# A selective-scan layer and an up-sampled MLP: sums of one pair in three a step later, and GpSimd's product by C in place, in one pool of six buffers

## The chip, the core and the metric

The kernel runs on one core of one Trainium2 chip, in float32 throughout. The time is that of one execution on the device, in microseconds (us), as the median of several runs. Five engines work side by side, each through its own queue in order: TensorE (PE in the profile; PEld is its load of weights), VectorE (DVE), ScalarE (ACT), GpSimd (POOL) and SyncE (SP), which issues the DMAs. They are held together by semaphores: an instruction starts when the counters that it names have reached their values.

## What is computed

Two layers on an image batch `x` of 8 x 64 x 64 x 96. The first normalises, projects to 192 channels, convolves, and runs a selective scan over the 4096 places of an image, in four directions (`K` = 4) and with 16 states for each channel. This is where nearly all the time goes:

```python
def step(h, inp):
    ul, dl, Bl, Cl = inp
    dA = jnp.exp(dl[..., None] * A)
    h = dA * h + (dl * ul)[..., None] * Bl[:, :, None, :]
    y = jnp.einsum('bkdn,bkn->bkd', h, Cl)
    return (h, y)
```

The four directions are added up, normalised, gated and projected back. The second layer is `x + conv(gn(x))`: an up-sampling by two through the frequencies, an MLP of 96, 384 and 96 channels with a quadratic in the middle, and a low-pass filter back to 64 x 64.

## The kernel before

**A tile** is one direction, 1024 places in a row, and 8 channels x 16 states = 128 partitions: a 128 x 1024 array. A chunk of 1024 places takes 24 tiles (`NT`), since 192 / 8 = 24; with 4 chunks, 4 directions and 8 images there are 3072 tiles, numbered through by the loop variable `i`. `t["i"]` is the place within the chunk, 0 to 23. Tiles whose place has remainder 2 by 3 are `by_pool`.

**What a tile goes through**, engine by engine:

- `fetch` (L1063, SyncE's queue): a DMA brings `dub`, the product of step and input, each channel copied to its 16 states (4 buffers).
- `product_b` (L1069, GpSimd): `bb = dub * br`, with B spread over the partitions (4 buffers).
- `decay` (L1075 on TensorE, L1082 on ScalarE): two matmuls spread the steps into `pd` in PSUM (2 buffers), and an exponential on ScalarE turns it in place into the decay.
- `scan` (L1089, VectorE): the recurrence itself. It writes over `pd`, or, where the tile is `by_pool`, into `h` in SBUF, of which there are 2 buffers.
- `product_c` (L1095): `hc = h * cr`. On VectorE right after the scan, or on GpSimd for the tiles `by_pool`. Both draw `hc` from one pool of 4 buffers.
- `hold` (L1108): the last column is copied to `carry` for the next chunk, by VectorE, or by ScalarE for the tiles `by_pool`. It is left out in the last chunk of a direction.
- `sums` (L1127, TensorE): the states are added up by matmuls with `sel_r` into `py`, one PSUM bank with one buffer. It is done for two tiles at a time, `a` and `a + 1` with `a` even, four matmuls in the source and eight in the profile, which has two records for each. After the pair with `j == 3` the earlier directions are added (L1139), ScalarE copies `py` out (L1160) and SyncE stores it.

**The order** is written by hand, with no scheduler: one pass of the loop at L1193 for each tile. In pass `i` the queues get: the fetch of tile `i + 6`; on GpSimd `product_c` of tile `i - 1` if it is `by_pool`, then `product_b` of tile `i + 3`; the decay of tile `i + 1`; the scan of tile `i`, then its `product_c` if it is VectorE's; its `hold`; a share of the side work; perhaps a filler matmul; and in odd passes the sums of the tiles `i - 3` and `i - 2`.

**Side work** is all that isn't the scan: the norms, convolutions, gates, projections, the MLP, and the preparation of the next chunk (`prepare`). `Side.advance` hands it out in small pieces, against a budget for each engine and pass (`CAPS`, 2.2 us of TensorE in a pass, up to 2.9 us saved up). The sums of a pair are charged to the budget of their pass as 0.95 us (`taken`). If less than 1.0 us of TensorE was given out in a pass, `turn_over` (L1101) adds a filler matmul into a spare bank.

**A cycle of six passes** therefore looks as follows, where a number is a tile's remainder by 6. Tiles 2 and 5 are GpSimd's. The pairs are (0, 1), (2, 3) and (4, 5). GpSimd gets the product of tile 5 in the next pass 0, and that of tile 2 in pass 3. TensorE gets, in this order: decay 2, sums of (4, 5) of the cycle before; decay 3; decay 4, sums of (0, 1); decay 5; decay 0, sums of (2, 3); decay 1. The sums of (4, 5) thus stand in front of decay 3, and need the product that GpSimd makes of tile 5.

Of the kernel before, what the change touches and what calls it, by code (L numbers as in the profile page):

```python
# [8 lines left out]
F32 = mybir.dt.float32  # L9
# [13 lines left out]
T = 1024  # L23
# [113 lines left out]
def kernel(ctx: ExitStack, tc: tile.TileContext, a: dict, out: bass.AP):  # L137
# [93 lines left out]
    sp = ctx.enter_context(tc.tile_pool(name="scan", bufs=3))  # L231
# [3 lines left out]
    side = Side(pss)  # L235
# [805 lines left out]
    tiles = []  # L1041
    for b in range(images):
        for k in (1, 0, 2, 3):
            order = range(NCH) if k < 2 else range(NCH - 1, -1, -1)
            for n, c in enumerate(order):
                got = {}
                for i in range(NT):
                    q, n8 = divmod(i, 8)
                    s, j = n8 % 2, n8 // 2
# [9 lines left out]
    def fetch(t):  # L1059
        assert t["got"]["ready"]  # L1060
        t["dub"] = sp.tile([128, T], F32, tag="dub", name="dub", bufs=4)
        g = t["g"]
        nc.sync.dma_start(  # L1063
            t["dub"], t["got"]["du"][None, 8 * g : 8 * g + 8, :].to_broadcast([NS, 8, T])
        )
# [18 lines left out]
    def scan(t):  # L1084
        step = 1 if t["k"] < 2 else -1
        pd = t["pd"]
        t["h"] = sp.tile([128, T], F32, tag="h", name="h", bufs=2) if t["by_pool"] else pd
        held = carry[:, t["g"] : t["g"] + 1]
        nc.vector.tensor_tensor_scan(  # L1089
            t["h"][:, ::step], pd[:, ::step], t["bb"][:, ::step], 0.0 if t["first"] else held, ALU.mult, ALU.add  # L1090
        )

    def product_c(t):
        t["hc"] = sp.tile([128, T], F32, tag="hc", name="hc", bufs=4)
        (nc.gpsimd if t["by_pool"] else nc.vector).tensor_tensor(t["hc"], t["h"], t["got"]["cr"], ALU.mult)  # L1095

    def turn_over():
# [14 lines left out]
    def parts(t):  # L1112

        o = y_dram[t["b"]][t["k"] % 2]
        q = t["q"]
        return [o[64 * q : 64 * q + 64, t["i0"] + MB * hf : t["i0"] + MB * hf + MB] for hf in range(2)]

    def sums(two):

        t0 = two[0]  # L1120
        if t0["j"] == 0:
            t0["got"]["py"] = psy.tile([128, MB], F32, tag="py", name="py")
        py = t0["got"]["py"]
        for t in two:
            for hf in range(2):
                r0 = 64 * hf + 32 * t["s"]
                nc.tensor.matmul(  # L1127
                    py[r0 : r0 + 32],
                    sel_r[:, t["j"], :],
                    t["hc"][:, MB * hf : MB * hf + MB],  # L1130
                    start=(t["j"] == 0),
                    stop=(t["j"] == 3 and t["k"] == 0),
                    skip_group_check=True,
                )

        if t0["j"] == 3 and t0["k"]:

            add = d_diag[:, t0["q"], :] if t0["k"] == 1 else ident
            nc.tensor.matmul(py, add, t0["got"]["yp"], start=False, stop=True, skip_group_check=True)  # L1139

    def before(t):

        if t["k"] == 0:
            return
        yp = t["got"]["yp"] = sp.tile([128, MB], F32, tag="yp", name="yp", bufs=2)
        if t["k"] == 1:
            q = t["q"]
            src = [
                u_dram[t["b"]][1][64 * q : 64 * q + 64, t["i0"] + MB * hf : t["i0"] + MB * hf + MB]
                for hf in range(2)  # L1150
            ]
        else:
            src = parts(t)
        for hf in range(2):
            nc.sync.dma_start(yp[64 * hf : 64 * hf + 64], src[hf])

    def store(t):
        yield dict(act=0.7)
        yq = sp.tile([128, MB], F32, tag="yq", name="yq", bufs=1)
        nc.scalar.copy(yq, t["got"]["py"])  # L1160
        yield {}
        for hf, part in enumerate(parts(t)):
            nc.sync.dma_start(part, yq[64 * hf : 64 * hf + 64])
        if t["q"] == Q3 - 1:
            if t["k"] == 3:
                summed.add((t["b"], t["i0"] // T))
            elif t["k"] == 2 and t["i0"] == 0:
                summed.add((t["b"], "even"))

    LEAD, FETCH = 3, 6  # L1170

    with tc.manual_schedule():
        side.queue = [bp.open("setup")]
        side.drain()
        constants_in()
        start, rest = front(0)
        side.queue = start[:-4]
        side.drain()
        side.queue = start[-4:] + [(8, 0, constants_of_scans), (8, 0, constants_of_mlp)]
        side.drain()  # L1180
        side.urgent = prepare(0, tiles[0]["k"], tiles[0]["i0"], tiles[0]["got"])
        side.queue, rest = rest[:4], rest[4:]
        while side.urgent or side.hurried:
            side.advance({e: (2 * most, 2 * most) for e, (_, most) in Side.CAPS.items()}, 2, 0)
        n = len(tiles)
        for i in range(FETCH):
            fetch(tiles[i])
            if i >= FETCH - LEAD:
                product_b(tiles[i - FETCH + LEAD])
        decay(tiles[0])  # L1190
        begin, *side.later = prepare(0, tiles[NT]["k"], tiles[NT]["i0"], tiles[NT]["got"])
        total = 1
        for i in range(n + 4):  # L1193
            t = tiles[i] if i < n else None
            at = i % (NT * NCH * K)
            if t and t["i"] == 0:
                b = t["b"]
                if at == 0:
                    y_dram[b] = [dr.tile([DI, L], F32, tag=f"y{o}", name=f"y{o}") for o in range(2)]
                    side.begun, hasty = 0, sum(item[1] for item in rest) if b == 0 else 0  # L1200
                    side.queue += rest
                    down, end = [], []
                    if b:
                        keep = {}
                        side.queue += tail(b - 1, keep)
                        up, down, end = mlp(b - 1, keep)
                        side.queue += up
                    if b + 1 < images:
                        start, rest = front(b + 1)
                        side.queue += start[:2] + [i for two in zip(down, start[2:10]) for i in two] if b else start[:10]  # L1210
                        side.queue += start[10:] + rest
                        rest = []
                    else:
                        side.queue += down
                    side.queue += end
                    total = sum(item[1] for item in side.queue)
                if b == images - 1 and at == NT * NCH * (K - 1):
                    keep = {}
                    side.queue += tail(b, keep, pairs=False)
                    total = 0  # L1220

            ahead = 4 if i < 2 * NT else 8
            if (i + ahead) % NT == 0 and i + ahead + NT < n:
                nxt = tiles[i + ahead + NT]
                begin, *side.later = prepare(nxt["b"], nxt["k"], nxt["i0"], nxt["got"])
                side.urgent.append(begin)

            if i == 2:
                side.urgent.append(begin)
            if i == 4 or i and i % NT == 0:  # L1230
                side.urgent += side.later
                side.later = []
            if t and t["i"] % 8 == 4:
                before(t)
            if i + FETCH < n:
                fetch(tiles[i + FETCH])
            if 0 < i <= n and tiles[i - 1]["by_pool"]:
                product_c(tiles[i - 1])
            if i + LEAD < n:
                product_b(tiles[i + LEAD])  # L1240
            if i + 1 < n:
                decay(tiles[i + 1])
            if t:
                scan(t)
                if not t["by_pool"]:
                    product_c(t)
                hold(t)
            ends = i % 2 == 1 and 3 <= i <= n + 2
            adds = ends and tiles[i - 2]["j"] == 3 and tiles[i - 2]["k"]
            side.advance(  # L1250
                Side.CAPS,
                2 if not total or side.begun < max(hasty, total * at / 290) else 0,
                0 if 7 <= i % NT <= 21 else 1,
                0.95 * (bool(ends) + bool(adds)),
            )
            turn_over()
            if ends:
                sums(tiles[i - 3 : i - 1])
                if tiles[i - 2]["j"] == 3:
                    side.stores.append([g := store(tiles[i - 2]), next(g)])  # L1260
        up, down, end = mlp(images - 1, keep)
        side.queue += up + down + end
        side.drain()
# [89 lines left out]
```

## Time and profile before

| what | value |
|---|---|
| runs (3) | 11121.33, 11125.21, 11125.94 us; median 11125.21 |
| the profiled execution | 11107.68 us, its span 11105.8 us |
| granted TensorE clock, mean | 0.982 |
| share of 16 DMA engines, queue of SyncE | 86.5% |
| ScalarE busy | 5910.6 us (53%) |
| scans, L1089, all four forms | 3072, 7163.7 us, 392.6 us idle before them |
| sums, L1127, matmuls | 12288 records, 1715.0 us |
| copies to `carry` by ScalarE, L1108 | 768, 172/182/193 ns (least/median/most) |

The span of a profile runs from the first to the last instruction; what lies around it is 1.9 us here. "Busy" is time in which an engine executes; "idle before" is the time that the engine stood before the instructions of a group, and the name behind the arrow is the instruction whose end let it go on, as inferred from the semaphores. A wait for several semaphores is put down to the one that came last.

### The profile page before, as it was taken

The page shows a single profiled execution, that of the slowest core. Times are in us where ns is not written, and L with a number is a line of the kernel's source. Part 1 is how long each engine was busy: PE and PEld are TensorE (multiplying, and loading weights), DVE is VectorE, ACT ScalarE, POOL GpSimd, SP SyncE. Part 2 cuts the span into 40 slices and gives each one's busy share as a digit, 9 for nine tenths or more (in the row PEclk, how much of TensorE's full clock was granted, in tenths as well). Part 3 has the DMA queues.
Part 4 walks back from the last instruction along what each step waited for, and adds up shares of the span by engine and source line. Part 5 has one row for each costly group of instructions (what it writes and reads, how often), then busy time and mean ns, then how long its engine had stood idle before and what let it go on. Part 6 is the DMA issues. An engine that isn't in the chain of part 4 may idle for free. (4 is left out here: it accounts for less than half of the span.)

```text
span 11105.8 us, 137238 instructions
## 1 busy us (share of the span) xinstructions
PE 9967.9 (90%) x45020; PEld 3204.6 (29%) x45020; DVE 10207.5 (92%) x7702; ACT 5910.6 (53%) x8218; POOL 10179.6 (92%) x4674
## 2 busy tenths in 40 slices
PE   8898888989889998999889998899988989889988
PEld 2222222322233222332223322233222332223325
DVE  6999999999999999999999999999999999999990
ACT  5455445656455564555545555455554655545543
POOL 5999999999999999999999999999999999999990
PEclk9999999999999999999999999999999999999998
DMA  6888898898988989888988989889898898988981
GB/s 174 215 208 224 209 231 209 217 227 232 233 209 216 225 231 225 212 218 224 240 217 215 224 221 244 209 219 225 217 243 210 217 228 218 247 206 216 227 214 48
DMA packets 1044463, 2401.27 MB, mean 216 GB/s; under 512 B 293820, under 2 KB 314556, under 8 KB 1043752
## 3 DMA queue, kind: packets, MB, share of 16 engines
q1 hardware_dynamic: 1042776, 2391.45, 86.5%
q8 instruction: 361, 5.91, 0.2%
q14 instruction: 350, 2.87, 0.1%
q10 hardware_dynamic: 976, 1.04, 0.0%
HBM read 1929.05 MB, written 328.73 MB: 203 GB/s over the span
## 5 line engine op out<-in xcount | busy, mean ns | idle before, releaser
L1069 POOL TENSOR_TENSOR bb<-dub,br 128x1024 f32<-128x1024 f32 x3072 | 7173.5, 2359 | 208.4 <-DMA dub<-du 149.2
L1082 ACT ACTIVATE pd<-pd,neg_a 128x1024 f32<-128x1024 f32 x3072 | 3340.7, 1088 | 4533.0 <-PE pd L1075 4489.8
L1075 PE MATMUL pd<-dl,sel_b 64*128 64x512 f32 x12288 | 3512.7, 645 | 987.2 <-DVE carry L1108 649.2
L1089 DVE TENSOR_TENSOR_SCAN pd<-pd,carry,bb 128x1024 f32<-128x1024 f32 x1536 | 3610.3, 2350 | 262.2 <-ACT carry L1108 127.9
L1095 POOL TENSOR_TENSOR hc<-h,cr 128x1024 f32<-128x1024 f32 x1024 | 2413.9, 2357 | 352.6 <-DVE h L1089 300.7
L1095 DVE TENSOR_TENSOR hc<-pd,cr 128x1024 f32<-128x1024 f32 x2048 | 2508.4, 1225 | 164.1 <-PE py L1127 20.0
L1075 PEld LDWEIGHTS pd<-dl,sel_b 64*128 64x128 f32 x12288 | 966.7, 186 | 3266.3 <-issue 1511.2
L1089 DVE TENSOR_TENSOR_SCAN h<-pd,carry,bb 128x1024 f32<-128x1024 f32 x768 | 1797.3, 2340 | 5.8 <-ACT pd L1082 5.6
L1127 PE MATMUL py<-hc,sel_r 128*32 128x512 f32 x12288 | 1715.0, 617 | 30.4 <-POOL hc L1095 30.2
L1089 DVE TENSOR_TENSOR_SCAN pd<-pd,bb 128x1024 f32<-128x1024 f32 x512 | 1172.5, 2290 | 98.6 <-ACT carry L1108 75.3
L1101 PE MATMUL idle<-sel_b,ident 128*128 128x512 f32 x1652 | 932.0, 646 | 8.0 <-DVE ty L720 5.9
L562 PE MATMUL pc<-pad,convr 96*128 96x512 f32 (+1 forms) x2304 | 858.3, 616 | 5.7 <-DVE e L585 3.6
L1089 DVE TENSOR_TENSOR_SCAN h<-pd,bb 128x1024 f32<-128x1024 f32 x256 | 583.6, 2280 | 26.0 <-ACT pd L1082 25.2
L1127 PEld LDWEIGHTS py<-hc,sel_r 128*32 128x32 f32 x12288 | 250.3, 109 | 1109.0 <-issue 854.5
L1031 POOL TENSOR_TENSOR u<-dl,u 128x512 f32<-128x512 f32 x384 | 485.0, 1271 | 79.2 <-DVE dl L1028 79.2
L862 PEld LDWEIGHTS p<-w2q,mq 128*100 128x100 f32 x4800 | 452.9, 168 | 274.6 <-issue 214.2
L855 PE MATMUL ph<-xu,w 96*128 96x500 f32 x960 | 504.9, 629 | 11.5 <-ACT mq L856 6.7
L862 PE MATMUL p<-w2q,mq 128*100 128x96 f32 x4800 | 511.5, 258 | 2.3 <-ACT mq L856 2.3
L562 PEld LDWEIGHTS pc<-pad,convr 96*128 96x128 f32 (+1 forms) x2304 | 266.3, 163 | 563.9 <-issue 552.8
L987 PE MATMUL px<-u,xp 64*64 64x512 f32 x1536 | 422.4, 627 | 2.4 <-issue 2.4
L1101 PEld LDWEIGHTS idle<-sel_b,ident 128*128 128x128 f32 x1652 | 249.8, 189 | 596.5 <-issue 522.4
L1012 PE MATMUL pv<-xd,dt_w 64*64 64x512 f32 x1536 | 394.4, 609 | 1.0 <-ACT xd L997 1.0
(153 smaller groups left out, 6707.9 us busy)
## 6 DMA issues: line engine op xcount, KB each, us to landing
dub<-du SPq DMA_DIRECT2D x3072, 512.0 KB
u<-u SPq DMA_DIRECT2D x256, 384.0 KB
du<-u SPq DMA_DIRECT2D x768, 128.0 KB
y<-yq SPq DMA_DIRECT2D x768, 128.0 KB
br<-xd SPq DMA_DIRECT2D x256, 256.0 KB
cr<-xd SPq DMA_DIRECT2D x256, 256.0 KB
yp<-y SPq DMA_DIRECT2D x384, 128.0 KB
yp<-u SPq DMA_DIRECT2D x192, 128.0 KB
```

The lines of the kernel that those rows point to most:

```text
L562: nc.tensor.matmul(t[rows].rearrange("p (i j) -> p i j", i=8), weights[:, cs], v["pad"][:, 8 * blk + kw : 8 * blk + kw + 8, kh : kh + H], ...
L855: nc.tensor.matmul(t[:, :px], w1[:, m, :], xu, start=True, stop=True)
L862: nc.tensor.matmul(t[:SIDE, C * i : C * i + C], sq[:, m, row], w2q[:, m, :], start=(m == 0), stop=(m == 2))
L987: nc.tensor.matmul(p[rows], xp[rows, k, q, :], v["u"][rows, q, :], start=(q == 0), stop=(q == 2), skip_group_check=True,)
L1031: nc.gpsimd.tensor_tensor(v["u"][:, q, :], got["dl"][:, q, :], v["u"][:, q, :], ALU.mult)
L1069: nc.gpsimd.tensor_tensor(t["bb"], t["dub"], t["got"]["br"], ALU.mult)
L1075: nc.tensor.matmul(pd[:, MB * hf : MB * hf + MB], sel_b[rows, 4 * t["s"] + t["j"]].rearrange("p n c -> p (n c)"), t["got"]["dl"][rows, t[" ...
L1082: nc.scalar.activation(pd, pd, AF.Exp, scale=neg_a[:, t["k"], t["g"] : t["g"] + 1])
L1089: nc.vector.tensor_tensor_scan(t["h"][:, ::step], pd[:, ::step], t["bb"][:, ::step], 0.0 if t["first"] else held, ALU.mult, ALU.add)
L1095: (nc.gpsimd if t["by_pool"] else nc.vector).tensor_tensor(t["hc"], t["h"], t["got"]["cr"], ALU.mult)
L1101: nc.tensor.matmul(p, ident, sel_b[:, 0:4].rearrange("p j n c -> p (j n c)"), start=True, stop=True)
L1127: nc.tensor.matmul(py[r0 : r0 + 32], sel_r[:, t["j"], :], t["hc"][:, MB * hf : MB * hf + MB], start=(t["j"] == 0), stop=(t["j"] == 3 and t ...
```

## The change

`product_c` of the tiles `by_pool` no longer writes to a buffer of its own, but over `h`. The two buffers of `h` and the four of `hc` become one pool of six, from which each tile takes exactly one: at its scan if it is `by_pool`, at its product otherwise. So a tile takes over the buffer of the tile six before it; until now the tile four before it (for `hc`).

The sums are no longer tied to odd passes. A new function says which pair is due in a pass: a pair `a` is summed in pass `a + 3` as before, but in pass `a + 4` if `a % 6 == 4` and its second tile has `j != 3`. These are the pairs (4, 5) of the cycle above, but for the last pair of a chunk: 3 of the 12 pairs in a chunk. The charge of 0.95 us and the store move along. The rest is the loop's own bookkeeping.

```diff
     def scan(t):
         step = 1 if t["k"] < 2 else -1
         pd = t["pd"]
-        t["h"] = sp.tile([128, T], F32, tag="h", name="h", bufs=2) if t["by_pool"] else pd
+
+        t["h"] = sp.tile([128, T], F32, tag="hc", name="h", bufs=6) if t["by_pool"] else pd
...
     def product_c(t):
-        t["hc"] = sp.tile([128, T], F32, tag="hc", name="hc", bufs=4)
+        t["hc"] = t["h"] if t["by_pool"] else sp.tile([128, T], F32, tag="hc", name="hc", bufs=6)
         (nc.gpsimd if t["by_pool"] else nc.vector).tensor_tensor(t["hc"], t["h"], t["got"]["cr"], ALU.mult)
...
+    def pair_due(i):
+        for lag in (3, 4):
+            a = i - lag
+            if a >= 0 and a % 2 == 0 and a + 1 < n:
+                late = a % 6 == 4 and tiles[a + 1]["j"] != 3
+                if lag == 3 + late:
+                    return tiles[a : a + 2]
+        return None
...
-            ends = i % 2 == 1 and 3 <= i <= n + 2
-            adds = ends and tiles[i - 2]["j"] == 3 and tiles[i - 2]["k"]
+            two = pair_due(i)
+            ends = two and two[1]["j"] == 3
+            adds = ends and two[1]["k"]
             side.advance(
                 Side.CAPS,
                 2 if not total or side.begun < max(hasty, total * at / 290) else 0,
                 0 if 7 <= i % NT <= 21 else 1,
-                0.95 * (bool(ends) + bool(adds)),
+                0.95 * (bool(two) + bool(adds)),
             )
             turn_over()
-            if ends:
-                sums(tiles[i - 3 : i - 1])
-                if tiles[i - 2]["j"] == 3:
-                    side.stores.append([g := store(tiles[i - 2]), next(g)])
+            if two:
+                sums(two)
+                if ends:
+                    side.stores.append([g := store(two[1]), next(g)])
```

More of the change, by code (lines that the diff above doesn't have):

```diff
@@ L1168, in store @@
                 summed.add((t["b"], "even"))
+    n = len(tiles)
     LEAD, FETCH = 3, 6
@@ L1184 @@
             side.advance({e: (2 * most, 2 * most) for e, (_, most) in Side.CAPS.items()}, 2, 0)
-        n = len(tiles)
         for i in range(FETCH):
```

## The prediction

> **What bounds the kernel now.** First the page's busy times, then the same for the stretch in which the loop runs (from 135 to 10836 us of the span):
>
> ```profile
> PE 9967.9 (90%) x45020; PEld 3204.6 (29%) x45020; DVE 10207.5 (92%) x7702; ACT 5910.6 (53%) x8218; POOL 10179.6 (92%) x4674
> ```
> ```profile
> core 0: us, PE busy (x) PEld busy (x) DVE busy (x) ACT busy (x) POOL busy (x), PEclk, DMA share, GB/s
> 135.00:10836.00 10701.00, 9633.16 (x43368) 3023.21 (x43368) 10151.34 (x7584) 5756.36 (x7965) 10140.68 (x4634) 0.99 0.89 222
> ```
>
> In the loop VectorE stands idle for 550 of 10701 us and GpSimd for 560. Which of the two sets the pace is told by who waits for whom. The view of waits, for DVE and for POOL:
>
> ```profile
> DVE pd L1089 <- ACT carry L1108: 203.2, 414, 3.6
> DVE pd L1089 <- ACT pd L1082: 113.8, 238, 8.0
> DVE pd L1089 <- POOL bb L1069: 40.2, 38, 2.3
> DVE hc L1095 <- PE py L1127: 20.0, 8, 4.2
> ...
> POOL hc L1095 <- DVE h L1089: 300.7, 335, 6.4
> POOL bb L1069 <- DMA dub<-du: 149.2, 115, 6.0
> ```
>
> VectorE waits 41 us for GpSimd (40.2 and 0.8 in a smaller row), GpSimd over 300 us for VectorE. In half of the tiles `bb` is ready over 5 us before its scan, counted from the rows of the trace. So VectorE's chain sets the pace, and its idle time is the path. It has two homes, in the groups of DVE by form:
>
> ```profile
> L1089 DVE TENSOR_TENSOR_SCAN pd<-pd,carry,bb 128x1024 f32<-128x1024 f32 x1536 | 3610.3, 2350 | 262.2 <-ACT carry L1108 127.9 <-ACT pd L1082 91.9 <-POOL bb L1069 39.7
> L1095 DVE TENSOR_TENSOR hc<-pd,cr 128x1024 f32<-128x1024 f32 x2048 | 2508.4, 1225 | 164.1 <-PE py L1127 20.0 <-DVE pd L1089 4.6 <-PE p L862 0.5
> ```
>
> **The change, part by part.** Times are of the profiled execution (span 11105.8 us, 11107.7 us in all); the median of the runs is 17.5 us more, and I carry the difference over to it.
>
> *VectorE's product loses a wait.* With four buffers, the product of tiles 0 and 4 of the six waits for its own scan and, because of the buffer, for TensorE; that of tiles 1 and 3 for its scan alone. The timeline shows both kinds, a scan and its product each:
>
> ```profile
> 5011.16 2.34 DVE L1089 TENSOR_TENSOR_SCAN pd<-pd,carry,bb 128x1024 f32<-128x1024 f32 x1
> 5013.53 1.22 DVE L1095 TENSOR_TENSOR hc<-pd,cr 128x1024 f32<-128x1024 f32 x1
> ...
> 5020.92 2.35 DVE L1089 TENSOR_TENSOR_SCAN pd<-pd,carry,bb 128x1024 f32<-128x1024 f32 x1
> 5023.37 1.23 DVE L1095 TENSOR_TENSOR hc<-pd,cr 128x1024 f32<-128x1024 f32 x1
> ```
>
> The first product starts 0.03 us after its scan's end, the second 0.10, though nothing was late. Over all rows the 1024 with one wait idle 34.5 ns each, 35.3 us together; the other 1024 have the rest of 164.1, 128.8 us. In the compiled order of the changed kernel no product of VectorE waits for TensorE, since the buffer of six tiles ago has been read before the decay that the scan waited for. 122 at chunk starts keep a second wait (for `cr`'s DMA), 7 us over the short gap. Gain 128.8 - 35.3 - 7 = **86 us**, 20 of them real waits. It is not swallowed behind: the scans that follow (tiles 1 and 5) idle only 17.0 and 8.1 us in all, and their decays are done 0.86 and 1.11 us earlier (medians). Bounds: 20 (if the 0.07 us is the price of something else) and 94.
>
> *Sums of (4, 5) leave the place before decay 3.* What they do there at worst:
>
> ```profile
> 6914.88 3.00 POOL L684 TENSOR_TENSOR ty<-ty,ye 96x512 f32<-96x512 f32 x2
> 6917.84 2.34 POOL L1095 TENSOR_TENSOR hc<-h,cr 128x1024 f32<-128x1024 f32 x1
> 6920.23 1.05 PE L1127 MATMUL py<-hc,sel_r 128*32 128x512 f32 x4 [2.01 <-POOL hc L1095]
> 6922.39 1.09 ACT L1082 ACTIVATE pd<-pd,neg_a 128x1024 f32<-128x1024 f32 x1 [5.92 <-PE pd L1075]
> 6923.58 2.36 DVE L1089 TENSOR_TENSOR_SCAN pd<-pd,carry,bb 128x1024 f32<-128x1024 f32 x1 [3.06 <-ACT carry L1108]
> ```
>
> Side work on GpSimd makes the product late, the sums hold up TensorE, the decay queued behind them holds up ScalarE, and the scan comes 3.06 us late. I sorted the scans' idle time by place: 32.1, 47.1 and 36.3 us at places 9, 15 and 21 of the chunk, whose decays stand behind the moved sums; 4.3, 48.7 and 31.4 at 6, 12 and 18, alike in all but that. Gain 115.5 - 84.4 = **31 us**; the 38 moved pairs that really waited for GpSimd have 26 of it. At most every place becomes like 6: 103. On the other side the sums now stand before decay 4. Scans of remainder 4 idle 19.6 us, those of 1, with sums before their decays already, 17.0; I take nothing. If they became like remainder 3 (187.2 us), three quarters of 168 would be lost, 126; against that speaks 0.77 us of median slack, and that the product is then a whole pass (3.5 us) older. The moved 0.95 us of budget shifts side work and its DMAs by a pass or so; no sum issues a DMA, pairs with a store (`j == 3`) stay, nothing passes another fetch in SyncE's queue, and the work after the loop is the same.
>
> *TensorE's decays gain waits.* VectorE no longer vouches for TensorE's progress, and 1713 decays carry a second wait in place of 1520. At remainder 0 such decays start 0.21 us after the product, others 0.05 to 0.12, so some 0.1 us, on the path where the scan waits for its decay (half of them). Loss between 0 and 19, I take **5**.
>
> *GpSimd's product in place.* The trace before has no such form. Three rows near it, each least/median/most in ns:
>
> ```profile
> L224 POOL TENSOR_TENSOR convr<-convr,w_cin x9: 578/581/588, 14.4 to 18.8; 96x192 f32<-96x192 f32 x9
> L1031 POOL TENSOR_TENSOR u<-dl,u x384: 1250/1268/1327, 90.2 to 10700.6; 128x512 f32<-128x512 f32 x192
> L684 POOL TENSOR_TENSOR ty<-ty,ye x128: 1507/1524/1562, 1535.4 to 10850.3; 96x512 f32<-96x512 f32 x128
> ```
>
> A line through 1268 (512 columns, over its second operand) and 2354 (1024, L1095, a buffer of its own) gives 589 at 192; L224, in place over its first operand, took 581. So **0**. L684, in place too, took 1.20 times L1031; it reads `ye` with a stride, by L684's source, which I hold for the reason. At that ratio: 0.47 x 1024 = 483 us of GpSimd.
>
> [...]
>
> *GpSimd waits for ScalarE.* Over `h`, the product must wait until `hold` has read it (744 in the compiled order), and `hold` is queued on ScalarE behind the next decay. Set against the rows of before, 365 of 768 products would start later, by 0.37 us on average, 134 us in all. Behind it queue the next `bb`s; the cover is their lead of 5 us, and in those cases GpSimd was ahead. Alone **0**, bounds 0 and 134.
>
> *Coupling.* GpSimd does the same work in less time. Of its 560 us, 162 wait for DMAs in the loop (149.2 and 13.3 for `pad`), 398 are slack. With 112 us less, the 41 us that VectorE waits become 41 x 398/286 = 57, +16; with the 134 taken off too, 41 x 398/152 = 107, +66. I take **+25**.
>
> Sum: -86 - 31 + 5 + 0 + 25 = -87. 11107.7 - 87 = 11020.7 for a profiled execution, **11038 us** as the median.
>
> [...]
>
> **Rivals.**
> - *GpSimd becomes the bound*, no change: sums gain 0, waits on TensorE cost 19, coupling 66: -86 + 19 + 66 = -1, 11124 us. For it: 92% on both, and a new wait. Against it: its lead.
> - *In place is dear*, slower: at L684's ratio GpSimd's loop is 10141 + 483 + 162 of DMA = 10786 us at least, against 10701: +85, and up to 134 more for ScalarE: 11210 to 11344, middle 11277. It decides once a product costs 0.29 us more (10141 + 162 + 1024 x 0.29 = 10600, what VectorE's chain then needs), and is slower than before beyond 0.39. Against it: L224.
> - *The 0.07 us stays*, the change doing less than it says: -20 - 31 + 5 + 10 = -36, 11089. Against it: one-wait products start after 0.03 us everywhere.
>
> **How the numbers follow.** Forecast 0.64, with a range of its own of 10970 (86, and two thirds of the 103) to 11080; beyond it 0.05; 0.07 us stays 0.07; GpSimd bound 0.13; in place dear 0.11. About 0.2%, 22 us, is what a measurement of this kernel can tell from no change. Faster: 0.64 + 0.05 + 0.07 + 0.04 of the GpSimd case = 0.80; within: 0.09; slower: 0.11. The range, 10970 to 11115, leaves out 0.05 below and 0.16 above.
>
> **What would show it.** Right: idle before VectorE's products falls from 164 to some 42 us with busy times unchanged; idle before the scans falls from 393 to some 365; TensorE's sums wait less for GpSimd; L1095's rows on POOL stay near 2357 ns, with more idle before them, now released by ScalarE. Wrong: those rows longer than 2.6 us; scans waiting over 100 us for `bb`; products still 0.10 us after their scans; scans of remainder 4 idling like those of 3.

## The result, and the profile after

The changed kernel takes 11154.81 us (median of 14 runs), the kernel before 11121.63 (14 runs): a ratio of **1.0034**, 95% interval 1.0025 to 1.0043. By the ratio it is slower by about 38 us, where 87 us of gain had been forecast. The profiled execution took 11164.6 us, its span 11162.8, which is 57 us more than that of before.

VectorE's two groups, in the view of groups by form (line, engine, operation, tiles, shapes, count, then busy us and mean ns, then idle us before and what ended it):

```profile
L1090 DVE TENSOR_TENSOR_SCAN pd<-pd,carry,bb 128x1024 f32<-128x1024 f32 x1536 | 3611.0, 2351 | 342.9 <-ACT carry L1109 133.7 <-ACT pd L1082 119.9 <-POOL bb L1069 84.9
L1096 DVE TENSOR_TENSOR hc<-pd,cr 128x1024 f32<-128x1024 f32 x2048 | 2508.5, 1225 | 70.6
L1090 DVE TENSOR_TENSOR_SCAN h<-pd,carry,bb 128x1024 f32<-128x1024 f32 x768 | 1797.4, 2340 | 0.9 <-POOL bb L1069 0.6 <-ACT pd L1082 0.2
L1090 DVE TENSOR_TENSOR_SCAN pd<-pd,bb 128x1024 f32<-128x1024 f32 x512 | 1173.3, 2292 | 179.2 <-ACT carry L1109 94.8 <-ACT pd L1082 76.8 <-POOL bb L1069 4.2
L1090 DVE TENSOR_TENSOR_SCAN h<-pd,bb 128x1024 f32<-128x1024 f32 x256 | 583.6, 2280 | 5.0 <-POOL bb L1069 4.5
```

Idle before the products fell from 164.1 to 70.6 us: 93.5 us, all that was there to win. Idle before the scans, in the four other rows, rose from 392.6 to 528.0 us: 135 us. Their busy times are what they were. So the change did its work at the products and lost more than that at the scans. The timeline shows the products as the prediction wanted them; each now starts 0.04 us after its scan's end:

```profile
5010.37 2.34 DVE L1090 TENSOR_TENSOR_SCAN pd<-pd,carry,bb 128x1024 f32<-128x1024 f32 x1
5012.75 1.23 DVE L1096 TENSOR_TENSOR hc<-pd,cr 128x1024 f32<-128x1024 f32 x1
...
5013.95 2.35 DVE L1090 TENSOR_TENSOR_SCAN pd<-pd,carry,bb 128x1024 f32<-128x1024 f32 x1
5016.34 1.23 DVE L1096 TENSOR_TENSOR hc<-pd,cr 128x1024 f32<-128x1024 f32 x1
```

The view of waits (us in all, times, longest) for DVE and for POOL:

```profile
DVE pd L1090 <- ACT carry L1109: 228.4, 423, 4.4
DVE pd L1090 <- ACT pd L1082: 196.7, 300, 8.0
DVE pd L1090 <- POOL bb L1069: 89.2, 49, 3.5
...
POOL h L1096 <- ACT carry L1109: 310.3, 328, 3.7
```

The first two rows are both waits for a decay, since ScalarE's copy to `carry` directly follows it; they grew from 317 to 425 us (for the scans into `h`, whose rows aren't shown, the same waits fell from 31 us to almost none). Waits for `bb` grew from 40 to 89. GpSimd is now released before its product by ScalarE's copy, as forecast. Its product's row on the page reads 2360 ns, against 2357 before.

Where along the chunk VectorE waits, added up from the rows of the trace by a tile's place (us of idle before its scan, one profiled execution each; "in place" is the second kernel below, without the late pairs):

| places | decay stands behind | before | in place | changed |
|---|---|---|---|---|
| 9, 15, 21 | the sums that the change moves away | 115.5 | 111 | 80 |
| 10, 16, 22 | those sums' new place | 9 | 9 | 73 |
| 1, 7, 13, 19 | sums of (2, 3), not moved | 17 | 30 | 68 |
| 3 | sums of the chunk's last pair, not moved | 75 | 82 | 107 |
| 0, 6, 12, 18 | side work alone | 132 | 148 | 188 |
| the remaining 9 | other mixes | 43 | 65 | 11 |

The three places that the change was to help were helped by 31 to 36 us. The loss is in the others, all but the last row.

Which input of a late scan came last can be read from the same rows. If `bb` came before the decay, the decay was late either because TensorE was (the exponential starts within 0.15 us of the end of its matmuls) or because ScalarE was still held up after that. Idle before scans by what came last, in us:

| came last | before | in place | changed |
|---|---|---|---|
| decay, TensorE late | 299 | 328 | 354 |
| decay, ScalarE late | 53 | 69 | 85 |
| `bb` | 38 | 44 | 85 |

So on balance the late pairs add some 26, 16 and 41 us of waiting, and TensorE's queue is about a third of it.

### The profile page after: what moved, and what is told of

Same layout as the page of the kernel before. It is cut to its first block, busy times and chain, and to the rows that moved or that the text cites. A ratio compares the mean times of both kernels' runs of the same rounds, so it can differ in the third digit from the quotient of the medians.

```text
span 11162.8 us, 135880 instructions
## 1 busy us (share of the span) xinstructions
PE 10053.5 (90%) x45032; PEld 3228.3 (29%) x45032; DVE 10218.2 (92%) x7702; ACT 5909.4 (53%) x8218; POOL 10184.7 (91%) x4674
## 4 chain that ended last, share of the span: by engine, by line
PE 27%; DVE 25%; POOL 18%; issue 15%; DMA 9%; ACT 5%; SPq 1%; DVEq 0%; POOLq 0%; ACTq 0%
DVE pd L1090 16%; POOL bb L1069 13%; PE pd L1075 10%; DMA dub<-du 6%; PE py L1128 4%; PE pc L562 3%; ACT pd L1082 3%; DVE hc L1096 3%; DVE h L1090 3%; POOL h L1096 3%; PE ph L855 2%; PE px L987 1%; PE p L862 1%; POOL u L1031 1%; PE idle L1102 1%
## 5 line engine op out<-in xcount | busy, mean ns | idle before, releaser
L1096 POOL TENSOR_TENSOR h<-h,cr 128x1024 f32<-128x1024 f32 x1024 | 2416.5, 2360 | 421.8 <-ACT carry L1109 310.3
L1096 DVE TENSOR_TENSOR hc<-pd,cr 128x1024 f32<-128x1024 f32 x2048 | 2508.5, 1225 | 70.6
L1128 PE MATMUL py<-hc,sel_r 128*32 128x512 f32 x8192 | 1662.2, 615 | 0.0
L1128 PE MATMUL py<-h,sel_r 128*32 128x512 f32 x4096 | 1116.2, 624 | 22.5 <-POOL h L1096 22.5
```

Of the source, the lines that this page charges most:

```text
L1128: nc.tensor.matmul(py[r0 : r0 + 32], sel_r[:, t["j"], :], t["hc"][:, MB * hf : MB * hf + MB], start=(t["j"] == 0), stop=(t["j"] == 3 and t ...
```

## The experiments

Every ratio is against runs of the kernel before on the same chip, and differences in per cent are taken from these ratios. Lines of code shift a little from kernel to kernel.

### Each half of the change alone

The product in place and the pool of six, with every pair in pass `a + 3`:

```diff
-                late = a % 6 == 4 and tiles[a + 1]["j"] != 3
+                late = False
```

> The changed kernel with every pair summed in pass a+3 again: only the product in place and the pool of six. Theory 1 (the loss comes from the sums' new place before decay 4, and the rest of the change is a gain): idle before VectorE's products 70 us, idle before scans near 393, so about 11121 - 85 = 11035 us. Theory 2 (the loss comes from GpSimd's product waiting for ScalarE's copy, which makes bb and the sums of the last pair late): idle before products 70, but before scans some 480, waits of VectorE for bb near 90, so 11100 to 11125 us. Theory 3 (whatever VectorE gains it gives back, since GpSimd has as much to do): 11121, within 10.

Measured: 11089.31 us, ratio 0.9971 (0.9962 to 0.9981). **A gain**, of 32 us, and the fastest kernel in this study that leaves nothing out. Its groups on DVE, from the page:

```profile
L1090 DVE TENSOR_TENSOR_SCAN pd<-pd,carry,bb 128x1024 f32<-128x1024 f32 x1536 | 3609.9, 2350 | 287.7 <-ACT carry L1109 154.8
L1096 DVE TENSOR_TENSOR hc<-pd,cr 128x1024 f32<-128x1024 f32 x2048 | 2507.8, 1225 | 70.6
L1090 DVE TENSOR_TENSOR_SCAN pd<-pd,bb 128x1024 f32<-128x1024 f32 x512 | 1172.6, 2290 | 104.0 <-ACT carry L1109 78.3
```

The products' idle is gone here too. With the scans into `h` (17.8 and 36.4 us) the scans idle 445.9 us, 53 more than before. So of 94 us won, 53 came back as waits at the scans in the same execution. The sign is theory 1's, the size is not: 32 us and not 85.

The late pairs alone, with `h` and `hc` in their old buffers (2 and 4) and GpSimd's product written to its own:

```diff
-        t["h"] = sp.tile([128, T], F32, tag="hc", name="h", bufs=6) if t["by_pool"] else pd
+        t["h"] = sp.tile([128, T], F32, tag="h", name="h", bufs=2) if t["by_pool"] else pd
...
-        t["hc"] = t["h"] if t["by_pool"] else sp.tile([128, T], F32, tag="hc", name="hc", bufs=6)
+        t["hc"] = sp.tile([128, T], F32, tag="hc", name="hc", bufs=4)
```

> The kernel before with the late pairs alone: h keeps its two buffers and hc its four, the product on GpSimd has its own output, pairs (4, 5) are summed a pass later. Theory 1 (the sums' new place costs): idle at places 9, 15, 21 falls by some 37 us, at 10, 16, 22 it rises by some 64, and the products of VectorE keep their second wait, now with a few real waits more: 11150 to 11180 us. Theory 2 and 3 (the new place is harmless or a gain): 11090 to 11121 us.

Measured: 11209.76 us, 1.0082 (1.0067 to 1.0097), **slower by 91 us**. Its products idle 184.3 us, 20 over those of before: with four buffers the later sums give 384 products of remainder 3 a second wait as well (17.7 us of idle before, 51.6 now), while those of remainder 4 idle 17 us less. The rest of the loss, 62 us, is at the scans. That is more than theory 1 had, although places 10, 16 and 22 rose by less, from 9 to 43 us. The changed kernel is 0.63% slower than the one with the product in place alone, which is 70 us by the ratios, give or take 15, and 65 by the medians, 11154.8 against 11089.3. So the late pairs cost 65 to 70 us on top of the product in place and 91 alone: in sign the halves agree with the whole, but their costs don't simply add up.

### GpSimd's new wait for ScalarE

The copies to `carry` left out for the tiles `by_pool`, in the changed kernel and, as a control, in the kernel before (`carry` is set to zero once at the start):

```diff
-        if t["last"]:
+        if t["last"] or t["by_pool"]:
             return
```

> The changed kernel without ScalarE's copies of the last column: tiles by_pool pass no state on to the next chunk (carry stays zero for them), so that GpSimd's product in place has nothing to wait for but the scan. Theory 2 (the wait for ScalarE's copy is what costs): waits of VectorE for bb back to some 45 us, idle of place 3 back to 75, 11055 to 11095 us. Theory 1 or 3: within 20 us of the changed kernel, 11135 to 11155.

> The kernel before without ScalarE's copies of the last column (tiles by_pool pass no state on): the control for the run above, since it takes the same 140 us of work from ScalarE, which is busy for 53%, and no wait from GpSimd. All theories: 11105 to 11125 us.

Measured: 11144.41 us (1.0024, 1.0015 to 1.0033) and 11115.4 us (0.9998, 0.9988 to 1.0007). Without anything to wait for but the scan, the changed kernel gains 0.10%, and the kernel before gains 0.02% from the same copies, so the wait is worth some 9 us, which the intervals hardly tell from none. Theory 2 falls. Without the copies GpSimd still idles 368 us before its product, against 422 with them, now for the scan itself, and VectorE waits as long for `bb`:

```profile
DVE pd L1091 <- POOL bb L1070: 93.5, 59, 3.4
...
POOL h L1097 <- DVE h L1091: 363.3, 408, 5.8
```

### The sums and their charge, taken apart

The late pairs do two things: the matmuls move, and so does their charge of 0.95 us against the budget of side work. First the sums late, the charge in the old, odd passes:

```diff
+            was = i % 2 == 1 and 3 <= i <= n + 2
...
-                0.95 * (bool(two) + bool(adds)),
+                0.95 * (bool(was) + bool(was and tiles[i - 2]["j"] == 3 and tiles[i - 2]["k"])),
```

> The changed kernel, with the sums in the changed passes, but charged to the budget of side work in the old ones (odd passes). The late pairs cost 65 us (changed kernel 11155 against 11089 without them). Theory 1a (the matmuls' own place before decay 4 costs): nothing changes, 11145 to 11165 us. Theory 1b (the moved charge costs, because it lets side work pile up before decay 3 and shifts all that follows): most of the 65 us come back, 11090 to 11115 us. Half of each: 11120.

Then the reverse, on the kernel with the product in place: sums in the old passes, and the charge where the changed kernel has it (`pair_due` with the rule of lateness on for the charge alone).

```diff
-                0.95 * (bool(two) + bool(adds)),
+                0.95 * (bool(charged) + bool(charged and charged[1]["j"] == 3 and charged[1]["k"])),
```

> The counterpart: product in place and pool of six, all sums in the old passes, but the charge of 0.95 us moved to the passes in which the changed kernel has them. Theory 1a: 11080 to 11100 us, like the kernel with the product in place alone (11089). Theory 1b: 11130 to 11160 us.

Measured: 11262.16 us, 1.0136 (1.0122 to 1.015), and 11192.44 us, 1.0072 (1.0059 to 1.0084). Neither theory holds. Against the kernel with the product in place (0.9971), moving the sums alone costs 1.65%, the charge alone 1.01%, and both together, as in the changed kernel, 0.63%. The two belong together, and moved together they still cost. The waits of DVE, sums alone:

```profile
DVE pd L1090 <- ACT pd L1082: 254.7, 395, 8.0
DVE h L1090 <- ACT pd L1082: 65.1, 61, 5.8
```

and charge alone:

```profile
DVE pd L1090 <- ACT carry L1109: 335.2, 496, 5.7
```

By remainder of six, the scans' idle shows where: with the sums alone that of remainder 4 rises from 19 us to 173 (sums and a full ration of side work stand before decay 4); with the charge alone that of remainder 3 rises from 194 to 318 (the same before decay 3). In both, work beyond the ration in front of a decay shows up as idle time at that decay's scan.

The table by places can now be split too. At place 3 and at places 1, 7, 13 and 19 the charge alone gives 107 and 72 us, as in the changed kernel (107 and 68), and the sums alone 86 and 34, near the kernel with the product in place (82 and 30): this loss comes with the moved charge. At places 0, 6, 12 and 18 the sums alone give 185 us and the charge alone 161, against 148 without either and 188 with both: here it is more the sums.

### How much of VectorE's time counts

To learn why 94 us of idle were worth only 32, a known cost was put on VectorE at the place of the wait that had gone: a copy of 64 columns after the products of tiles 0 and 4, in the kernel with the product in place and in that of before.

```diff
                 hold(t)
+                if i % 6 in (0, 4):
+                    nc.vector.tensor_copy(scrap, t["h"][:, :64])
```

> The kernel with the product in place and all sums in the old passes (11089 us), with a copy of 64 columns added on VectorE behind the products of tiles 0 and 4 of six, 1024 of them, to a scrap buffer: a known cost on VectorE at the very place where the second wait was taken away. The profile tells what it costs (copies of one column take 0.148 us, so 0.2 us each, some 200 us). Theory A (VectorE's time counts in part only, since the rest is handed on as waits for the decays): the kernel loses as much of it as it won of the 94 us, 36%, so some 70 us, 11160 us, and idle before scans falls by the rest. Theory D (VectorE's time counts in full, and the product in place loses 60 us by something else, such as the clock): 11270 to 11300 us.

> The same 1024 copies in the kernel before, as the other point of the slope. Theory A: a larger share counts than above, as VectorE is then later against the others: 11120 + 80 to 150 us. Theory D: 11120 + 180 to 210 us.

The copy's own rows in the first of the two (the view of one tile; least/median/most ns, then the scans in the groups of the same kernel):

```profile
L1265 DVE COPY scrap<-pd x1024: 211/214/216, 124.3 to 10890.2; 128x64 f32<-128x64 f32 x171
```
```profile
L1091 DVE TENSOR_TENSOR_SCAN pd<-pd,carry,bb 128x1024 f32<-128x1024 f32 x1536 | 3610.0, 2350 | 254.5 <-ACT carry L1110 142.7 <-ACT pd L1083 70.2 <-POOL bb L1070 37.9
```

The copies overlap their neighbours: VectorE's busy time grew from 10208.4 to 10341.7 us, so they cost 133 us, 0.13 each. The time rose to 11163.97 us (1.0049, 1.0036 to 1.0061), 0.78% or 87 us: **65%** of the cost. In the kernel before, 11216.26 us (1.0094, 1.0078 to 1.0109) and 105 us: **79%**. The rest is taken from waits: in the first kernel idle before the scans fell from 446 to 404 us. Both times are near theory A's, but partly by luck: the copies cost 133 us and not 200, and more than its 36% counted, though less than all. If time taken away counted like time put on, which no run shows, the 94 us should have brought 61 to 74. They brought 32 (21 to 42 by the interval), so as an estimate the product in place costs some 30 to 40 us elsewhere. Three terms can be bounded. The wait for ScalarE is worth some 10 us. The second wait that 227 more decays carry on TensorE in this kernel (1747 records of a separate wait, 1520 before) is at most 21: released by VectorE, a decay starts 0.145 us after it with such a wait and 0.054 without (medians). And 12 us more than before are lost where a copy of side work on ScalarE (L810) holds up a decay, as shown further down. How much of each counts in time no run takes apart; that stays open.

### TensorE's queue, without fillers and with another ration

The filler matmuls left out of the kernel with the product in place:

```diff
-        if side.spent < 1.0 and side.free:
+        if False:
```

> Product in place, sums in the old passes, and no filler matmuls (1652 records, 932 us of TensorE). VectorE's products idle 94 us less with the product in place, but the kernel gained only 34. Theory A (the rest is given back at TensorE, whose queue in front of the decays is now too long): TensorE busy falls to some 82%, idle before scans falls below 393 us, 11020 to 11060 us. Theory B (given back at GpSimd, as waits for bb): 11080 to 11095 us. Theory C: TensorE's granted clock falls without fillers, its matmuls take longer and the kernel is slower, over 11110 us.

Measured: 11205.56 us, 1.0081 (1.0067 to 1.0095): theory C. First the kernel with the product in place and fillers, then without, in the groups of PE:

```profile
L1075 PE MATMUL pd<-dl,sel_b 64*128 64x512 f32 x12288 | 3516.2, 645 | 923.9 <-DVE carry L1109 596.4 <-DVE hc L1096 274.9 <-DVE h L1090 37.6
```
```profile
L1075 PE MATMUL pd<-dl,sel_b 64*128 64x512 f32 x12288 | 3742.4, 683 | 1513.2 <-DVE carry L1109 950.8 <-DVE hc L1096 402.9 <-DVE h L1090 145.4
```

The granted clock falls from 0.982 to 0.934, the decays' matmuls get 6% longer, and the scans idle 580 us. What was to relieve the queue lengthened it, so this run doesn't tell A from B.

A second try left the fillers and only dealt the ration out differently, 1.25 us of charge for the pairs (4, 5) and 0.80 for the others:

```diff
-                0.95 * (bool(two) + bool(adds)),
+                (1.25 if i % 6 == 1 else 0.80 if i % 6 in (3, 5) else 0.95) * bool(two) + 0.95 * bool(adds),
```

> Product in place, all sums in the old passes, but the pairs (4, 5) are charged 1.25 us and the others 0.80, so that less side work stands before decay 3 and more before decays 1 and 5; the sum over a cycle stays. Theory A (the waits that took the place of the ones removed are decays late in TensorE's queue): idle before scans of remainder 3 falls from 194 us to some 150, those of 1 and 5 rise by 20: 11060 to 11080 us. If the queue before the decays doesn't matter: 11089, within 10.

Measured: 11125.99 us, 1.0014 (1.0005 to 1.0023), 0.43% slower than with even charges: a miss. Idle at remainder 3 hardly fell (194 to 190 us: place 3 lost 33 and places 9, 15 and 21 gained 29), and that at remainder 0 rose from 148 to 222. Here less work in front of one decay was more in front of another, and the even ration is the better of the two. The clock was 0.977 in this run, against 0.982; what that is worth isn't separated.

### GpSimd's share of the loss

Last, the changed kernel and its half with the product in place, both without GpSimd's product of step and input, the side work after which VectorE used to wait for `bb`:

```diff
-            nc.gpsimd.tensor_tensor(v["u"][:, q, :], got["dl"][:, q, :], v["u"][:, q, :], ALU.mult)
```

> Product in place, all sums in the old passes (11089 us), without GpSimd's product of step and input (L1031, 384 products, 485 us of GpSimd), the clump of side work after which VectorE waits for bb; the input goes into the scan without its step. Control for the next. VectorE waited 44 us for bb, so about 45 us less: 11030 to 11060.

> The changed kernel (11155 us) without the same products. It lies 65 us above the kernel with the product in place alone. Theory G (some 40 of the 65 are GpSimd's: the late sums make VectorE wait 85 us for bb in place of 44): 20 to 35 us above the control. Theory P (the 65 come from TensorE's queue alone, and the waits for bb follow from it): still 55 to 75 us above the control.

Measured: 11040.24 us (0.992, 0.9904 to 0.9936) and 11079.92 us (0.9958, 0.9944 to 0.9973). The late pairs cost 40 us here (0.38%, with an uncertainty of some 0.2%), against 65 to 70 with GpSimd's work in place; that is between the two theories. The row for `bb` among the waits of DVE, control first, then the changed kernel:

```profile
DVE pd L1089 <- POOL bb L1068: 20.6, 14, 2.3
```
```profile
DVE pd L1089 <- POOL bb L1068: 33.1, 31, 3.0
```

With the load on GpSimd gone, the late pairs lengthen the waits for `bb` by 12 us, and with it by 44 (44.8 to 89.2). So some 25 of the 65 us seem to hang on GpSimd's clumps of side work, and some 40 to remain at the decays. The times alone hardly tell the two costs apart; the rows for `bb` do.

## Why the prediction was wrong

**The step that failed** is the second: "On the other side the sums now stand before decay 4 ... I take nothing", with the sentence after it, that the moved budget merely "shifts side work and its DMAs by a pass or so". The gain of this step was right: 31 us at places 9, 15 and 21, and 31 to 36 were measured. But the same places' successors, 10, 16 and 22, lost 64 us (9 to 73), and the other places together some 48 more (326 to 374). In all the late pairs cost 65 us in place of a gain of 31. That is 96 of the some 120 us between the forecast and the result; the other 24 are the product in place, which brought 32 where -86 + 5 + 25 had promised 56. The analogy that let me take nothing, that scans of remainder 1 with sums before their decays idle only 17 us, failed twice over: in the changed kernel remainder 4 idles 78 us and remainder 1 itself 68. Of the 73 us, 48 are decays that were late on TensorE. How that can look, in the changed kernel's timeline, at place 16 of a chunk (rows left out between); the clock of this stretch follows, from the view of windows (PEclk is the third last):

```profile
5807.46 1.92 PE L710 MATMUL pn<-sq,mean_w 96*96 96x512 f32 x2
...
5810.16 1.07 PE L1128 MATMUL py<-hc,sel_r 128*32 128x512 f32 x2
...
5811.17 1.59 PE L1075 MATMUL pd<-dl,sel_b 64*128 64x512 f32 x4
...
5812.82 1.09 ACT L1082 ACTIVATE pd<-pd,neg_a 128x1024 f32<-128x1024 f32 x1 [2.08 <-PE pd L1075]
...
5814.01 2.36 DVE L1090 TENSOR_TENSOR_SCAN pd<-pd,carry,bb 128x1024 f32<-128x1024 f32 x1 [1.30 <-ACT pd L1082]
```
```profile
5805.00:5814.10 9.10, 9.10 (x32) 2.21 (x28) 7.73 (x7) 3.40 (x4) 9.10 (x5) 0.62 0.84 214
```

TensorE is busy throughout and nothing holds it up: side work, then the moved sums, then the decay, which is 1.3 us late for its scan. The median slack of 0.77 us that I had put against this was the slack of a queue without the sums in it, and the sums alone take 1.05 us.

Another 21 of the 73 us are not TensorE's doing. They are seven waits of some 3 us at place 16, of which this is one, at full clock (rows left out between):

```profile
5896.22 1.13 PE L1075 MATMUL pd<-dl,sel_b 64*128 64x512 f32 x4
...
5899.78 0.59 ACT L810 COPY t1s<-p 100x512 f32<-100x512 f32 x1 [4.45 <-DMA t<-t1s]
...
5900.26 1.09 ACT L1082 ACTIVATE pd<-pd,neg_a 128x1024 f32<-128x1024 f32 x1
...
5901.45 2.30 DVE L1090 TENSOR_TENSOR_SCAN pd<-pd,bb 128x1024 f32<-128x1024 f32 x1 [2.99 <-ACT pd L1082]
```

The matmuls of the decay are done at 5897.35, but the exponential is queued on ScalarE behind a copy of side work that waits 4.45 us for a DMA. Such copies held up decays before too, mostly at place 20: 24 us in all before, 36 in the kernel with the product in place, 45 in the changed kernel, at places 16 and 19 there. With the charge alone moved they stand at 16 and 19 as well, with the sums alone they don't. So it is the moved charge that put them there, and "shifts side work and its DMAs by a pass or so" had a price of its own.

The first of the two stretches ran at a granted clock of 0.62; the changed kernel's clock is 0.975 on the whole, against 0.982, and TensorE was busy for 86 us more on 12 more records. Of the 48 us that TensorE's lateness cost at places 10, 16 and 22, 29 fell where the clock was not full throughout the 6 us before the scan, and 19 where it was. Over all scans, idle time rose from 325 to 407 us after a full clock, and stayed at 121 us after a lower one (in place against changed; with 10 us before the scan, 321 to 382 and 125 to 146). So most of the added waiting stands at full clock, and the lower clock isn't needed for such a loss: the kernel with the moved charge alone lost 1.01% at 0.984.

Point by point, the other steps:

- *VectorE's product loses a wait*, 86 us, bounds 20 and 94: right in the group, 93.5 us, and every product at 0.035 us; the 7 us for `cr`'s DMA didn't come. The sign that goes with it, idle falling "to some 42 us", doesn't follow from the sum, which leaves 164 - 86 = 78; 70.6 were measured. Wrong in what it is worth: "it is not swallowed behind" looked only at the very next scan. Of a cost at this place 65 to 79% count in time, and the kernel with this half alone won 32 us.
- *TensorE's decays gain waits*, 5 us: not measured in time. At 0.145 against 0.054 us, 193 more of them are 18 us at most.
- *GpSimd's product in place*, 0: right, 2357 ns at the median (2333 to 2442), before 2354 (2330 to 2448). So over `h` or into a buffer of its own, the product took the same time to 3 ns. The line through L224 was the right neighbour, and L684's 1.20 was not of its being in place; that its stride made it, as I held, no run shows. The rival "in place is dear" ended up on the right side of the time for a cause that isn't there.
- *GpSimd waits for ScalarE*, 0: right within some 10 us, although 310 us of idle are now put down to that copy. Without the copies most of it is idle for the scan: 368 us in all, against 422.
- *Coupling*, +25: the waits for `bb` grew by 49 us in the changed kernel, but only by 5 in the kernel with the product in place, whose VectorE had gained the same 94 us. So it wasn't VectorE's speed that brought them, as that step had it, but the late pairs.
- *Idle time, not busy time, as the path*: right in kind. The runs went by waits: 32 us won by a change in waits alone, 65 lost by another, busy times of VectorE within 11 us.
- *What would show it*: of the four signs of being wrong none came true (2360 ns for the rows, 94 us of waits for `bb`, products at 0.035 us, remainder 4 at 78 us against 187), and yet the kernel was slower. The telling sign was on the other list: idle before the scans, which was to fall to 365 us and rose to 528.

## What to carry to other kernels

Where an engine's queue is filled by hand against a ration, moving an instruction means to check the whole segment of the queue in front of the next deadline, at its new place as closely as at its old, and to move its charge with it. A change that is the sum of a gain and a loss shows both only when each half is run alone: here the half with fewer buffers' waits is the better kernel (0.9971). And idle time won on a pacing engine (94 us here) is worth what the next waits leave of it. A padded copy of known cost gives a first figure for that, though not the whole answer: here it promised 61 to 74 us, and 32 came.

## What the runs showed of the hardware

- A second semaphore to wait for, long satisfied, cost VectorE 0.07 us for each product (0.104 against 0.0345 us after the scan), 71 us over 1024 of them. There the wait for the scan stood in a separate instruction ahead of the product, which ended 0.06 us after the scan. The changed kernel keeps such an instruction before 122 products, but for semaphores that were satisfied while the scan still ran, and these start after 0.035 us like all others.
- The same on TensorE: a decay released by VectorE started 0.145 us after it where a separate wait instruction stood before the decay (800 of them in the kernel before) and 0.054 us where none did (334).
- Fillers that cost TensorE 942 us kept its clock up in the kernel with the product in place: without them the granted clock fell from 0.982 to 0.934, from 135 to 10836 us of the span 1386 us at half clock against 321 (added up from the trace's clock records), and the kernel was 1.1% slower. In the run without fillers TensorE has 258 idle gaps over 2 us in the loop, 27 of them over 3 us, and 259 stretches at half clock, of one to five times 3.41 us; with fillers 55 gaps are over 2 us, and there are 70 such stretches. So in these two runs more gaps over 2 us go with a lowered clock; how long a gap, or how many, it takes, they don't show.
